# A four-layer graph network on one core: 166 loads moved to ScalarE's DMA queue, and four other orders of transfers and sums

## The chip, the cores and the metric

The kernel runs on one core of one Trainium2 chip. The metric is the device time of one execution in microseconds (us), taken as the median of several executions. Three executions of the kernel before gave 2234.57, 2238.84 and 2247.07 us.

The core's engines are TensorE (PE in the profile; PEld is its loading of weights), VectorE (DVE), ScalarE (ACT), GpSimd (POOL) and SyncE (SP). Each engine works through its own instructions in order. Transfers (DMAs) are started by instructions too: an engine that starts one only issues it, and 16 DMA engines move the bytes. In this kernel SyncE does nothing but issue transfers, GpSimd issues the others, and ScalarE, before the change, issues none.

## The reference

N = 2708 nodes, D = 512 features, `adj` a symmetric matrix of zeros and ones with about 16 ones in a row. Four layers, each in the form x = layernorm(x + layer(x)):

```python
deg = max(sum(adj != 0), 1)
x = ln(x + relu((dinv*(adj + I)*dinv @ x + x) @ W0 + b0))   # dinv = rsqrt(deg)
x = ln(x + (dis*adj*dis @ x) @ W1.T + b1)                   # dis = (deg + 1e-8)**-0.5
x = ln(x + gat(gat(x, W2[0]), W2[1]))
x = ln(x + adj @ (x @ W3 by heads) + b3)

def gat(x, W):
    Wh, Ws = split(x @ W, 2)
    a = softmax(Wh @ Ws.T, axis=-1) * adj
    return leaky_relu(a @ Wh + x)
```

The softmax runs over all 2708 columns, and only then is the result masked by `adj`, so the scores are needed in full but the product `a @ Wh` only where `adj` has ones.

## The kernel before, in words

**Tiling.** Nodes come in 22 blocks of 128 (the last has 20) and in six chunks of columns, four of 512, one of 384 and one of 276 (`CH`). The layers 0, 1 and 3 (class `Fast`) multiply by the adjacency: its bytes are loaded (`load_bytes`), ScalarE converts them to float (`m<-at` in the profile), and TensorE multiplies them with x (`acc<-m`). Attention (class `Attention`, L1632 ff.) works on scores transposed: for a chunk of 512, 384 or 276 queries it makes 22 tiles of scores, one for each block of keys.

**One chunk of attention.** `walk` (L2531) makes the scores. Chunks 0 to 3 of the first attention layer and 0 to 2 of the second do it by seven products instead of eight for two tiles (`pair_steps`, L2103): these need sums of halves of the weights (`s1`, `s2`, `s4`, kept in memory by `keep_sums` and loaded again by `load_sums`, L2047, tile group `s<-sums`) and sums of halves of the chunk's own columns (`t1`, `t2`, `t4`, made on VectorE by `sum_moving`, L2067). Their matmuls are `spx` and `spy`; ScalarE copies the results out of the accumulators into pages `s`, `u` and `v`, and VectorE adds them. The other chunks multiply plainly (`scores`, L2210, matmul `sp<-xs`). The chunk's own columns, four pages `xs`, are loaded by `load_moving` (L2200).

When a chunk's scores are there, the maximum is taken, and `soften` (L2306) is called once for each block while the next chunk's scores are made: VectorE subtracts the shift, ScalarE takes the exponential three blocks later, VectorE adds it to the sum and multiplies with the mask, and SyncE stores the tile to memory (`pairs<-s`). Mask bytes come by `load_mask` (L2291, `a<-mask`), four blocks (`DC`) in a page.

Then `fetch` (L2364) has GpSimd gather the few rows that each query needs (`g<-pairs,givers`, an indirect DMA), `weigh` sums them on TensorE (`acc<-g`), and `end` adds the query's own row `xr` (loaded by `load_rows`, L2391) and, in the second layer, the row `x` that the layer began with (`ch.first`, loaded in `fetch`).

**What sets the order.** `Attention.layer` (L2552) is an order written out by hand. The steps of a chunk are counted by n: at n = 15 the following chunk's `xs` are loaded, at n = 18 `sum_moving` is called for it, and `soften_next`, `greatest`, `weigh` and `copy_z` are spread over the steps. The first groups of the last layer (`early`, L645) run as filling in the tail of attention. A helper (`OrderedEngine`, L63) issues every instruction, so all have line L71 in the profile, and groups are told apart by their tiles. Instructions enter each engine's queue in the order of the program.

**Pages.** Nearly all tiles are pages of 2 KB in each of 128 partitions from one pool of 87. A page is used again when its last reader is done: a copy into a page that an earlier tile held waits for that tile's store to have read it. These waits, and those of a transfer for an earlier one with the same completion semaphore, are put in by the framework.

Of the kernel before, what the change touches and what calls it, by code (L numbers as in the profile page):

```python
# [12 lines left out]
U8 = mybir.dt.uint8  # L13
# [6 lines left out]
P = 128  # L20
N = 2708
D = 512
NB = 22
NP = NB * P
DC = D // P
BANK = 512
# [27 lines left out]
class Ordered:  # L54


    def __init__(self, tc):
        self.tc, self.last = tc, {}
        for name in ("tensor", "vector", "scalar", "gpsimd", "sync"):
            setattr(self, name, OrderedEngine(self, getattr(tc.nc, name)))  # L60
# [415 lines left out]
def blocks_of(k):  # L476

    c0, cw = CH[k]
    return [(c0 // P + q, q * P, min(P, cw - q * P)) for q in range(-(-cw // P))]
# [22 lines left out]
STREAMED = 4  # L502
# [8 lines left out]
def lists_of(i):  # L511

    if rows_of(i) <= QW:
        return [[QUARTERS * ONLY]] + [[t] for t in range(ONLY)]
    rest = [[QUARTERS * ONLY + t] for t in range(REST)]
    return rest + [[q * ONLY + t for q in range(QUARTERS)] for t in range(ONLY)]


def cost(columns):

    return 4 * columns / 2400
# [31 lines left out]
class Fast:  # L553
# [91 lines left out]
    def early(self, run):  # L645

        seq = run.seq
        yield True
        self.load(*seq[0])
        yield True  # L650
        self.load(*seq[1])
        self.prepare(*seq[0])
        yield True
        for t in range(4 * TWO):
            ly, k, g = seq[t]

            for later in seq[t + 2 if t == 0 else t + 6 : t + 7]:
                self.load_bytes(*later)
            if t < 2:
                self.attention.need(GROUPS[t + 2][1] - 1)  # L660
            if t == 1:
                for j in range(*GROUPS[3]):
                    ly.rows[j] = self.attention.made[j]
            self.load(*seq[t + 2])
            if t == 4:
                self.load_weights(ly)
            if t == 4 * TWO - 1:
                self.attention.need(GROUPS[4][1] - 1)
                for j in range(*GROUPS[4]):
                    ly.rows[j] = self.attention.made[j]  # L670
            self.prepare(*seq[t + 1])
            if g == 3:
                ly.begun[k] = []
            for n, j in enumerate(range(*GROUPS[g])):
                if t == 0:
                    self.multiply(ly, k, g, [j])
                else:
                    self.multiply(ly, k, g, ds=[n])
                if g == 3:
                    b = self.page(f"begun{k}_{n}")  # L680
                    self.nc.scalar.copy(b[:, : CH[k][1]], ly.acc[k][n][:, : CH[k][1]])
                    ly.begun[k].append(b)
                self.attention.advance(2 * cost(CH[k][1]))
                yield True
# [912 lines left out]
class Chunk:  # L1597


    def __init__(self, ly, k):  # L1600
        self.ly, self.k, self.cw = ly, k, CH[k][1]
        self.name = f"{ly.number}_{k}"
        self.blocks = blocks_of(k)
        self.s, self.masks, self.ends = {}, {}, []
        self.half = self.cw // 2
        self.seven = k in SEVEN[ly.number]
        self.part, self.complete, self.ready, self.top = {}, [], [], None
        self.softened = 0
        self.masks_ahead = 2 if k < STREAMED else 5
        self.fetched, self.rden = [], None  # L1610
        self.x, self.first = {}, {}
        self.rows = set()
        self.mv = None

        self.to_weigh = []
        for q, (i, _, _) in enumerate(self.blocks):
            ts = lists_of(i)
            self.to_weigh += [(q, t, t is ts[0], t is ts[-1]) for t in ts]
        self.to_fetch = [(q, t) for q, ts, _, _ in self.to_weigh for t in ts]
        self.first_fetch = self.to_fetch[0]  # L1620
# [11 lines left out]
class Attention:  # L1632
# [414 lines left out]
    def load_sums(self, ly, k):  # L2047

        for n, name in enumerate(("s1", "s2", "s4")):
            t = self.page(f"{name}_{ly.number}_{k}", FP, (P, 2, 2 * P))  # L2050
            self.nc.sync.dma_start(t, self.sums[ly.number][k][n])
            ly.sums[k][name] = [t[:, c, :] for c in range(2)]

    def replace(self, ly, k):
# [145 lines left out]
    def load_moving(self, ch):  # L2200

        ch.xt = []
        for c in range(DC):
            t = self.page(f"xs{ch.name}_{c}")
            self.nc.sync.dma_start(
                t[:, : ch.cw], self.k.turned[ch.ly.number][ch.k][:, c, :]
            )
            ch.xt.append(t)
# [80 lines left out]
        nc.scalar.copy(ch.shift[:, : ch.cw], ps[:, : ch.cw])  # L2289

    def load_mask(self, ch, g):  # L2291
        j0, j1 = g * DC, min((g + 1) * DC, NB)
        a = self.page(f"a{ch.name}_{j0}", U8, (P, DC, ch.cw))
        self.nc.sync.dma_start(a[:, : j1 - j0, :], self.k.masks[ch.k][:, j0:j1, :])
        for j in range(j0, j1):
            ch.masks[j] = a[:, j - j0, :]
# [9 lines left out]
    def soften(self, ch):  # L2306


        nc, v, cw = self.nc, ch.softened, ch.cw
        ch.softened += 1  # L2310
        if v < NB:
            n = rows_of(v)
            s = ch.s[v][:n, :cw]
            nc.vector.tensor_sub(s, s, ch.shift[:n, :cw])
        j = v - APART
        if 0 <= j < NB:
            s = ch.s[j][: rows_of(j), :cw]
            nc.scalar.activation(s, s, AF.Exp)
        j -= 1
        if j < 0:  # L2320
            return
        if j == NB - 1:
            ch.softened = SOFT
        if j == 0 and ch.k >= 2:
            while self.chunks[ch.k - 2].to_fetch:
                self.weigh(True)
        if j % DC == 0 and j + ch.masks_ahead * DC < NB:
            self.load_mask(ch, j // DC + ch.masks_ahead)
        n = rows_of(j)
        s = ch.s[j][:n, :cw]  # L2330
        if j == 0:
            ch.sum = self.page(f"sum{ch.name}")
            nc.vector.tensor_copy(ch.sum[:, :cw], s)
        else:
            nc.vector.tensor_add(ch.sum[:n, :cw], ch.sum[:n, :cw], s)
        nc.vector.tensor_mul(s, s, ch.masks.pop(j)[:n, :cw])
        to = ch.ly.pairs[ch.k % 2][j * P : j * P + n, :]
        if cw == BANK:
            four = [to.ap[0], (PAIR, 2), (P + D, 2), (1, P)]
            nc.sync.dma_start(  # L2340
                bass.AP(to.tensor, to.offset, four),
                ch.s[j][:n, :].rearrange("j (r b x) -> j r b x", r=2, b=2),
            )
            return
        nc.sync.dma_start(to[:, :P], ch.s[j][:n, :P])
        nc.sync.dma_start(to[:, P + D : D + cw], ch.s[j][:n, P:cw])
# [17 lines left out]
    def fetch(self, ch):  # L2364


        q, t = ch.to_fetch.pop(0)
        g = self.f.wide(f"g{ch.name}_{q}_{t}")
        i, _, w = ch.blocks[q]

        for b in (q, q + 1):
            self.load_rows(ch, b)
        if ch.ly.number == 1 and q not in ch.first:
            ch.first[q] = self.page(f"x1{ch.name}_{q}")
            self.nc.sync.dma_start(ch.first[q][:w], self.k.saved[1][i][:w])

        h = t // ONLY if t < QUARTERS * ONLY else (0, QUARTERS - 1)[q % 2]
        first, width = (P, D + (h + 1) * QW) if q % 2 else (h * QW, D + P - h * QW)
        self.nc.gpsimd.indirect_dma_start(
            out=g[:, :width],  # L2380
            out_offset=None,
            in_=ch.ly.pairs[ch.k % 2][:, :],
            in_offset=bass.IndirectOffsetOnAxis(ap=self.k.givers[:, i, t : t + 1], axis=0),
            element_offset=(q // 2) * PAIR + first,
        )

        begin = max(self.fetch_free, self.clock + (FIRST_LANDS if (q, t) == ch.first_fetch else 0))
        self.fetch_free = begin + 1.15
        ch.fetched.append((g, self.fetch_free + 6))

    def load_rows(self, ch, q):  # L2391
        if q in ch.rows or q >= len(ch.blocks):
            return
        ch.rows.add(q)
        i, _, w = ch.blocks[q]
        ch.x[q] = self.page(f"xr{ch.name}_{q}")
        given = self.k.saved[1] if ch.ly.number == 0 else self.k.between
        self.nc.sync.dma_start(ch.x[q][:w], given[i][:w])

    def fetch_ahead(self):  # L2400
        count = sum(len(c.fetched) for c in self.chunks)
# [150 lines left out]
    def layer(self, ly, chunks, fill):  # L2552
        f = self.f
        self.chunks, self.made = chunks, {}
        for k, ch in enumerate(chunks):
            old = chunks[k - 1] if k else None
            following = chunks[k + 1] if k + 1 < len(chunks) else None

            n = -1
            for what in self.walk(ch):  # L2560
# [22 lines left out]
                    f.packed(k - 1)  # L2583
                if following and n == 15:
                    self.load_moving(following)
                if following and following.seven and n == 18:
                    self.sum_moving(following)
                if not following and n in (5, 11, 19):
                    next(fill)
# [143 lines left out]
```

## Time and profile before

| | |
|---|---|
| median of three executions | 2238.84 us |
| profiled execution | 2238.97 us |
| its span in the trace | 2236.7 us (2.3 us lie outside) |
| matmuls, instructions in all | 10012, 30610 |
| transfers, moved | 310990 packets, 487.90 MB |
| mean granted TensorE clock | 0.992 |

A line of the page's first part gives each engine's busy us, its share of the span and its instructions. The stages are, from the trace: layers 0 and 1 to about 560 us; attention's projections, with the first chunk of scores, to about 800; its further chunks, the first scores from plain `xs` tiles at 801.9 and the last at 1888.3; gathers from 903.3 to 2030.0, the sums `acc<-g` to 2037.6; and the last layer to the end. Four of the groups that the change moves, by their tiles, with the number of transfers that SyncE issues: `s<-sums` 60, `xs<-t` 40, `xr<-x` and `xr<-y` 44, `x<-x` (in `fetch`) 22. SyncE issues 1224 transfers in all. Where a wait is shown, its columns are the engine, the tile that waited, the engine or transfer that ended the wait, us in total, times, and the longest.

### The profile page before, as it was taken

The numbers are of one execution on the slowest core, as the hardware profiler recorded it, in microseconds if no ns is written. First come the engines' busy times: TensorE is split into PE (matmuls) and PEld (weight loads), VectorE is DVE, ScalarE is ACT, GpSimd is POOL, SyncE is SP. The second block draws the span as 40 slices with busy tenths as digits, with TensorE's granted clock in tenths as the row PEclk, the third lists the DMA queues.
The fourth block names the chain that finished last, engine by engine and source line by source line (L and its number), as shares of the span: only waits on it lengthen the run. The fifth ranks groups of instructions, "written<-read, shape, count | busy, mean of one in ns | idle before, by whom it ended". The sixth has DMA issues, their size and how long they took to land.

```text
span 2236.7 us, 30610 instructions
## 1 busy us (share of the span) xinstructions
PE 2182.9 (98%) x10012; PEld 1576.6 (70%) x10012; DVE 1626.8 (73%) x3425; ACT 824.9 (37%) x1855; POOL 722.2 (32%) x827
## 2 busy tenths in 40 slices
PE   9999999999999999999999999999999998999997
PEld 6777788889887888765555666788743455577896
DVE  6777888897887869987758733459979698545744
ACT  7444363333333345433323422335423223342121
POOL 2333441111000000657465452000466666643000
PEclk9999999999999999999999999999999999999999
DMA  9976762222412855999799885674899899974221
GB/s 347 287 199 171 197 189 65 88 84 91 158 58 96 289 176 155 318 327 333 244 357 342 277 287 178 212 259 134 274 324 322 284 329 354 324 242 129 94 87 43
DMA packets 310990, 487.90 MB, mean 218 GB/s; under 512 B 37434, under 2 KB 178010, under 8 KB 310820
## 3 DMA queue, kind: packets, MB, share of 16 engines
q1 hardware_dynamic: 242164, 270.69, 36.5%
q0 software_dynamic: 68656, 215.15, 29.3%
q8 instruction: 81, 1.33, 0.2%
q14 instruction: 89, 0.73, 0.1%
HBM read 356.23 MB, written 162.76 MB: 232 GB/s over the span
## 4 chain that ended last, share of the span: by engine, by line
PE 94%; DVE 2%; issue 1%; DMA 1%; another core or an unknown queue 1%; ACT 0%; DVEq 0%; ACTq 0%; POOL 0%; POOLq 0%
PE acc L71 39%; PE sp L71 13%; PE spx L71 10%; PE spy L71 7%; PE mm L71 4%; PE mmx L71 3%; PE mmy L71 2%; PE z_0x L71 2%; PE wst L71 2%; PE z_0y L71 1%; PE mix L71 1%; PE wst_0x L71 1%; PE wst_1x L71 1%; PE z_1x L71 1%; PE wst_0y L71 1%
## 5 line engine op out<-in xcount | busy, mean ns | idle before, releaser
L71 POOL DMA_INDIRECT g<-pairs,givers x510 | 540.1, 1059 | 808.0 <-DMA xr<-x 235.3
L71 PE MATMUL acc<-m,xh 128*128 128x512 f32 (+4 forms) x1584 | 562.1, 376 | 6.7 <-ACT s L71 6.7
L71 PE MATMUL acc<-m,xl 128*128 128x512 f32 (+4 forms) x1584 | 548.1, 364 | 0.3 <-issue 0.3
L71 PEld LDWEIGHTS acc<-m,xh 128*128 128x128 f32 (+1 forms) x1584 | 287.4, 188 | 64.3 <-issue 17.2
L71 PEld LDWEIGHTS acc<-m,xl 128*128 128x128 f32 (+1 forms) x1584 | 287.7, 188 | 42.4 <-issue 3.6
L71 PE MATMUL sp<-xs,wst_sb 128*128 128x384 f32 (+2 forms) x960 | 301.5, 486 | 0.1
L71 PE MATMUL acc<-g 128*32 128x512 f32 (+1 forms) x1020 | 273.1, 613 | 7.2 <-issue 4.1
L71 PEld LDWEIGHTS sp<-xs,wst_sb 128*128 128x128 f32 x960 | 166.4, 183 | 133.0 <-issue 74.4
L71 ACT CAST m<-at 128x512 fp32r<-128x512 uint8 (+5 forms) x396 | 201.8, 569 | 111.4 <-DMA at<-mask 47.9
L71 DVE TENSOR_TENSOR sum<-sum,s 128x512 f32<-128x512 f32 (+4 forms) x252 | 156.9, 623 | 30.2 <-ACT s L71 22.9
L71 DVE TENSOR_TENSOR s<-s,a 128x512 f32<-128x512 f32 (+3 forms) x264 | 166.1, 629 | 9.1
L71 PEld LDWEIGHTS acc<-g 128*32 128x32 f32 (+1 forms) x1020 | 77.9, 136 | 134.4 <-issue 105.9
L71 DVE TENSOR_TENSOR top<-top,s 128x512 f32<-128x512 f32 (+3 forms) x240 | 149.4, 623 | 26.2 <-issue 15.3
L71 DVE TENSOR_TENSOR s<-s,shift 128x512 f32<-128x512 f32 (+3 forms) x264 | 161.2, 619 | 1.6 <-issue 1.3
L71 ACT COPY s<-sp 128x384 f32<-128x384 f32 (+2 forms) x112 | 52.5, 473 | 291.3 <-PE sp L71 153.9
L71 ACT ACTIVATE s<-s 128x512 f32<-128x512 f32 (+3 forms) x264 | 146.8, 581 | 13.5 <-DVE s L71 8.4
L71 POOL DMA_DIRECT2D x<-o x44 | 25.7, 590 | 325.2 <-DVE o L71 281.8
L71 ACT COPY s<-spx 128x256 f32<-128x256 f32 x210 | 77.5, 373 | 136.7 <-PE spx L71 98.1
L71 PE MATMUL spx<-xs,wst_sb 128*128 128x256 f32 x400 | 103.2, 383 | 0.0
L71 PE MATMUL mm<-w,ht 128*128 128x512 f32 (+1 forms) x240 | 99.1, 594 | 0.0
L71 DVE SCALAR_TENSOR_TENSOR xr<-acc,rden,xr 128x512 f32<-128x512 f32 (+1 forms) x44 | 32.8, 746 | 84.6 <-PE acc L71 65.2
L71 PEld LDWEIGHTS spx<-xs,wst_sb 128*128 128x128 f32 x400 | 76.0, 191 | 19.5 <-issue 7.4
(349 smaller groups left out, 3331.0 us busy)
## 6 DMA issues: line engine op xcount, KB each, us to landing
pairs<-s SPq DMA_DIRECT2D x168, 256.0 KB
at<-in_adj_t SPq DMA_DIRECT2D x84, 256.0 KB
pairs<-pairs SPq DMA_DIRECT2D x42, 512.0 KB
s<-sums SPq DMA_DIRECT2D x60, 256.0 KB
xres<-x POOLq DMA_DIRECT2D x44, 256.0 KB
x<-o POOLq DMA_DIRECT2D x43, 256.0 KB
pairs<-z_sb SPq DMA_DIRECT2D x42, 256.0 KB
pairs<-pairs SPq DMA_DIRECT2D x42, 256.0 KB
```

The source lines that it names most:

```text
L71: ins = call(*args, **kw)
```

## The change

It makes five edits.

- Four loads are issued in ScalarE's queue rather than SyncE's, at the same places of the program: the sums (`load_sums`), the chunk's columns (`load_moving`), the rows (`load_rows`) and the second layer's first rows (in `fetch`). That is 166 transfers.
- A mask page holds as many blocks as fit in it: four for chunks of 512, five for 384, seven for 276.
- The number of mask pages loaded ahead in chunks 4 and 5 goes from five to all but one: four and three.
- `early` loads the bytes of the last layer four groups ahead rather than six.
- `sum_moving` is called at n = 20, the last step of a chunk, rather than at n = 18.

```diff
         for t in range(4 * TWO):
             ly, k, g = seq[t]
-            for later in seq[t + 2 if t == 0 else t + 6 : t + 7]:
+            for later in seq[t + 2 if t == 0 else t + 4 : t + 5]:
                 self.load_bytes(*later)
...
-        self.masks_ahead = 2 if k < STREAMED else 5
+        self.together = BANK * DC // self.cw
+        self.masks_ahead = 2 if k < STREAMED else -(-NB // self.together) - 1
...
             t = self.page(f"{name}_{ly.number}_{k}", FP, (P, 2, 2 * P))
-            self.nc.sync.dma_start(t, self.sums[ly.number][k][n])
+            self.nc.scalar.dma_start(t, self.sums[ly.number][k][n])
...
             t = self.page(f"xs{ch.name}_{c}")
-            self.nc.sync.dma_start(
+            self.nc.scalar.dma_start(
                 t[:, : ch.cw], self.k.turned[ch.ly.number][ch.k][:, c, :]
             )
...
-        j0, j1 = g * DC, min((g + 1) * DC, NB)
-        a = self.page(f"a{ch.name}_{j0}", U8, (P, DC, ch.cw))
+        j0, j1 = g * ch.together, min((g + 1) * ch.together, NB)
+        a = self.page(f"a{ch.name}_{j0}", U8, (P, ch.together, ch.cw))
...
-        if j % DC == 0 and j + ch.masks_ahead * DC < NB:
-            self.load_mask(ch, j // DC + ch.masks_ahead)
+        if j % ch.together == 0 and j + ch.masks_ahead * ch.together < NB:
+            self.load_mask(ch, j // ch.together + ch.masks_ahead)
...
-            self.nc.sync.dma_start(ch.first[q][:w], self.k.saved[1][i][:w])
+            self.nc.scalar.dma_start(ch.first[q][:w], self.k.saved[1][i][:w])
...
-        self.nc.sync.dma_start(ch.x[q][:w], given[i][:w])
+        self.nc.scalar.dma_start(ch.x[q][:w], given[i][:w])
...
-                if following and following.seven and n == 18:
+                if following and following.seven and n == 20:
                     self.sum_moving(following)
```

## The prediction

> **What bounds the kernel now.** I read the page's busy shares first, then TensorE's waits, then the stage windows, then the places where TensorE stood still. The busy shares:
>
> ```profile
> span 2236.7 us, 30610 instructions
> PE 2182.9 (98%) x10012; PEld 1576.6 (70%) x10012; DVE 1626.8 (73%) x3425; ACT 824.9 (37%) x1855; POOL 722.2 (32%) x827
> ```
>
> TensorE is busy for all but 53.8 us of the span. The change touches no matmul, so that is the most that it can win directly. A second, smaller purse hangs on it: the granted clock stands at 0.5 for 6.8 us from 956.4, 1062.2, 1628.8 and 1895.1 and for 3.4 us from 1253.4, each time at a TensorE gap of 2.5 to 6.7 us. A window at half clock does half its work, so these cost about 4 x 3.4 + 1.7 = 15.3 us.
>
> TensorE's waits, columns: what waited, for what, us in total, times, longest:
>
> ```profile
> PE acc L71 <- ACT s L71: 6.7, 1, 6.7
> PE spx L71 <- issue: 5.7, 2, 4.9
> PE spx L71 <- ACT v L71: 4.8, 2, 3.9
> PE spy L71 <- issue: 4.6, 1, 4.6
> PE acc L71 <- issue: 4.4, 6, 1.4
> PE acc L71 <- DMA g<-pairs,givers: 2.7, 2, 1.8
> ```
>
> They are few and long. The windows (busy us and count of each engine, clock, DMA share, GB/s) tell where: 40 of the 54 us lie between 930 and 1990, in attention with its gathers.
>
> ```profile
> 930.00:1990.00 1060.00, 1020.46 (x4150) 646.59 (x4147) 748.60 (x1428) 360.05 (x814) 499.33 (x474) 0.99 0.85 287
> ```
>
> The 16 DMA engines are 85% busy here. I followed each gap to what ended it, in the rows of TensorE, ScalarE and SyncE, and sort them into three kinds:
>
> - **Stores that land late.** One at 1631.0 (4.60 us), and 0.74, 0.28 and 0.90 us at 1002.1, 1592.0 and 1602.7: 6.5 us, with 3.4 us of half clock after the first. In the timeline of SyncE, ScalarE and TensorE (start, duration, last idle time and releaser):
>
> ```profile
> 1617.71 7.88 SPq L71 DMA_DIRECT2D pairs<-s  x3
> ...
> 1630.58 0.37 ACT L71 COPY s<-spy 128x256 f32<-128x256 f32 x1 [10.51 <-DMA pairs<-s]
> ...
> 1631.01 2.07 PE L71 MATMUL spy<-xs,wst_sb 128*128 128x256 f32 x4 [4.60 <-issue]
> ```
>
> ScalarE's copy needs a page that `pairs<-s` is still reading; SyncE issued that store at 1617.71, after four `xs<-t`, an `xr<-y` and an `x<-x` (1611.52 to 1617.40), and in that stretch one issue of SyncE took 4.86 us. ScalarE idled 10.5 us and TensorE 4.6 of them: it had some 5.9 us of other work in hand, gather products among it.
> - **Gathers that come late**, 946.5, 1035.8, 1165.3, 1920.3, 1929.6: 0.92 + 0.57 + 1.07 + 1.44 + 1.81 = 5.8 us.
> - **Late signals.** At 957.6, 1063.3, 1253.2, 1314.6, 1317.3, 1363.4 and 1897.3 the matmul had ended, by its record, up to 10 us before ScalarE's copy began, with no other releaser in the trace: with smaller ones about 25 us, and 3 x 3.4 + 1.7 = 11.9 us of half clock. (Normally the copy follows 36 ns behind.) No part of the change is aimed at them.
>
> ScalarE's own waits for transfers, the edge that the change works on:
>
> ```profile
> ACT s L71 <- DMA pairs<-s: 15.4, 5, 10.5
> ...
> ACT v L71 <- DMA pairs<-s: 10.6, 4, 6.5
> ...
> ACT s L71 <- DMA a<-mask: 7.7, 3, 3.5
> ...
> ACT s L71 <- DMA xs<-t: 4.4, 2, 3.8
> ```
>
> **The moved loads: what SyncE gains.** 60 `s<-sums`, 40 `xs<-t`, 44 `xr` and 22 `x<-x` go to ScalarE's queue: 166 issues. By their rows an issue takes 0.40 to 0.47 us, say 166 x 0.45 = 75 us less of SyncE and 75 us more in ScalarE's queue. SyncE's time is not itself on the path: its longest waits are for results of VectorE (300.1 us for `s`). What counts is that stores no longer stand behind loads. In the 4.60 us case six loads stood ahead; a 256 KB load is 0.45 us of issue and, at the stage's 287 GB/s, about 0.9 us of transfer (estimates from these rows). I take the **late stores as gone: -6.5 - 3.4 = -9.9 us** (bounds -9.9 and 0), and the **late gathers as gone, -5.8** (bounds -5.8 and 0), since a gather starts only when the store before it has landed.
>
> Against this stands a bandwidth reading: from 1628 to 1636 the DMA engines are full (share 1.06), so that a load on another queue still takes the same engines. The Trainium skill says so too ("DMA: Bandwidth & Descriptors", section "Issuing engines are not separate DMA queues"): transfers started by different engines share the 16 DMA engines, and issuing from several saves only issue time. By it the two terms would be near 0 and the time 2239 plus ScalarE's cost; the row of 1617.71, where issue and order on SyncE are late in themselves, is why I don't go by it alone.
>
> **What ScalarE loses.** In the built programs the transfers of SyncE and ScalarE take eight completion semaphores in turn. So a load in ScalarE's queue waits for the transfer about eight earlier in program order, mostly a `pairs<-s`, a mask or a `pairs<-pairs` of SyncE, and ScalarE's copies and exponentials stand behind it; SyncE's next stores wait likewise for the loads, which are issued earlier, so that this way round costs little. In exchange 118 fewer of ScalarE's copies and exponentials wait for a transfer themselves (573 to 455). The trace of before shows no load on ScalarE, so I put each at its new place in ScalarE's order and looked up when the transfer that it would wait for landed before: ScalarE is held 75 us in 64 places, mostly in idle time that it has anyway. Blocks of over 7 us stand at 921.0 (11.0), 941.9 (7.1), 1151.7 (8.5), 1183.6 (9.6), 1278.0 (8.2), 1309.7 (7.9), 1619.5 (11.5), and at 1903.5 and 1972.4 where ScalarE has nothing to do. Followed on to TensorE (a product is 0.86 us; without gather products ScalarE has three products less a 0.37 us copy = 2.2 us of grace), ten of them reach it: 0.45 + 3.06 + 4.29 + 1.01 + 2.50 + 0.08 + 5.37 + 3.55 + 2.75 + 0.35 = 23.4 us. That is the upper end, with stores landing as they did behind 166 loads. Below nothing is excluded: a block only delays. The relief worked out above is 1.35 us for each load gone from ahead of a store; with two to six gone that is 2.7 to 8 us, as long as most of these blocks. So I take **+5 us** (bounds 0 and 23.4, to which four gaps of over 3 us could add 1.7 to 3.4 us of half clock each).
>
> **Mask pages.** Chunks of 384 columns go from six mask loads to five, of 276 from six to four: 6 issues of about 0.4 us off SyncE, which is not on the path, and one page and two pages fewer held. Each load is larger (up to 242 KB for 138 KB), issued three or four pages ahead. ScalarE's 7.7 us for `a<-mask` bound it: between -7.7 and +7.7 on ScalarE, of which TensorE sees a quarter (6.5 of 26.0 for the stores); I take **0**.
>
> **Bytes of the last layer, four groups ahead.** They are used later than they land by tens of us (`at3_1_2` landed at 1912 and is converted at 1961); the pages are free longer. **0**; if the cover were gone, a copy `m<-at` would wait a landing of 4.6 to 8.7 us once or twice.
>
> **Moving sums two steps later.** Six VectorE subtractions of 0.42 us for each of five chunks, with no transfers. The first chunk's end at 796.1 and are used at 807.1: 11 us of cover, less two steps (one pair, 6.05 us) leaves 5. **0**; without cover 2.5 us for each chunk, 12.7 in all. In exchange VectorE's chain of softmax goes on two steps longer undisturbed.
>
> **Sum.** 2238.97 - 9.9 - 5.8 + 5 = 2228.3; the profiled execution stands 0.13 us over the median, so **2228 us**. Its own spread, by the half of each term, is 2218 to 2236.
>
> **The rivals.** A difference of about 0.5% (11 us) is what can be told from no change here.
>
> *ScalarE blocked (slower).* The loads' waits for semaphores hold the copies, and TensorE pays what I followed to it: 2238.97 + 23.4 + two half clocks of 3.4 - 9.9 = 2259. It decides from the point at which half of the ten blocks are paid. For it: one block of ScalarE's queue in before (10.51 us) cost TensorE 4.6 us and half clock. Against it: of 26.0 us that ScalarE waited for stores TensorE saw 6.5.
>
> *Hidden anyway (no change).* Transfers are the limit (0.85 and 1.06 of the engines), stores land as before, ScalarE's blocks fall in its idle time: 2234 to 2243, 2239 at the middle. For it: SyncE's idle time, 300 us behind VectorE's `s` alone. This is also the case in which the change doesn't do what its words say.
>
> *Late signals move.* They are 25 + 11.9 us and depend on what falls together; if half go, 2228 - 18 = 2210; if they grow by half the case looks like the first rival.
>
> **How the numbers follow.** Forecast 0.45, ScalarE blocked 0.27, hidden 0.18, late signals fewer 0.10. Faster by over 0.5% (below 2227.6): over half of the first, all of the last, a little of the third: 0.38. Slower (above 2250): most of the second and the tail of the others: 0.28. Within: 0.34. Range 2206 to 2260: from the last rival's time to the ScalarE rival's.
>
> **What would show it.** Right: ScalarE's waits for `pairs<-s` shrink below 10 us, no gap of TensorE follows a store, gathers wait under 2 us. Wrong: ScalarE's idle time before copies ends at a DMA issue of its own queue, with TensorE gaps near 921, 941, 1151, 1278 or 1309; or the gaps of the first two kinds stay with the same sizes. If late signals differ by 15 us or more the forecast fails by a term that I set to 0.

## The result, and the profile after

The changed kernel takes 2271.34 us (median of five, 2261.77 to 2276.43), 1.0125 times the kernel before (95% interval 1.0096 to 1.0155): slower, and above the range of the forecast. Its profiled execution took 2271.34 us with a span of 2268.9 us. The page's first part after:

```profile
span 2268.9 us, 30484 instructions
PE 2192.1 (97%) x10012; PEld 1580.1 (70%) x10012; DVE 1626.1 (72%) x3425; ACT 822.8 (36%) x1855; POOL 715.0 (32%) x827
```

The span is 32.2 us longer. TensorE's busy time grew by 9.2 us, with the same 10012 matmuls, and its idle time by 23.0 (76.8 for 53.8). The first is the granted clock: without the window at the kernel's end it now stands at 0.5 for 61.2 us, where it stood for 30.6. In these windows TensorE was busy for 43.1 us, before for 23.9; half of the 19.2 more is 9.6, close to the 9.2. The second is in TensorE's waits (what waited, for what, us, times, longest):

```profile
PE wst_0x L71 <- ACT wst_sb L71: 10.3, 1, 10.3
PE acc L71 <- DMA g<-pairs,givers: 9.3, 5, 6.4
PE acc L71 <- issue: 9.2, 9, 2.4
PE spx L71 <- ACT v L71: 9.1, 3, 7.0
```

The two waits for ScalarE of 10.3 and 7.0 us are ahead of matmuls that had no gap before. ScalarE was busy 822.8 us in 2268.9, so it was not short of time. The window of the gathers holds less matmul work than before (4013 matmuls for 4150), with less clock (0.97 for 0.99) and no more DMA share (0.82 for 0.85):

```profile
930.00:1990.00 1060.00, 999.65 (x4013) 629.49 (x4014) 728.24 (x1381) 348.61 (x792) 481.73 (x462) 0.97 0.82 279
```

What ScalarE did is in its timeline at the 10.3 us wait. The columns are start, duration, engine, operation, tiles, and in brackets the idle time before and what ended it; ACTq is ScalarE's queue issuing a transfer:

```profile
1283.45 0.43 ACT L71 ACTIVATE s<-s 128x276 f32<-128x276 f32 x1 [0.83 <-DVE s L71]
1294.81 0.33 ACTq L71 DMA_DIRECT2D xr<-x  x1
1295.18 0.43 ACT L71 ACTIVATE s<-s 128x276 f32<-128x276 f32 x1 [11.29 <-DMA xt<-t]
1295.52 0.35 ACT L71 COPY wst_sb<-wst_0y 128x256 f32<-128x256 f32 x1
1295.77 0.38 ACT L71 COPY wst_sb<-wst_0x 128x256 f32<-128x256 f32 x1
```

The copies `wst_sb` have nothing to do with `xr<-x`. Their matmuls had ended at 1282.3 and 1283.2. But they stand behind the load in ScalarE's queue, and the load stands until a transfer of SyncE, `xt<-t`, has landed at 1294.8. SyncE issued it in this group:

```profile
1286.01 5.50 SPq L71 DMA_DIRECT2D xt<-t  x8
```

In the built program the load needs nothing of that `xt`. The two share a completion semaphore, which the `xt` had eight transfers earlier in the turn: the trace has number 101 for both, and the `xt` is the third of the eight, issued at 1287.04. The chain of work that ended last has the landing as one of its longest pieces, and two `pairs<-s` besides, the first of them behind `xr0_0_2` (start, us, what):

```profile
926.53 7.73 DMA pairs<-s
...
1003.36 7.20 DMA pairs<-s
...
1287.04 7.75 DMA xt<-t
```

The second place is the one that the prediction put at 921.0:

```profile
920.24 7.09 ACTq L71 DMA_DIRECT2D xs<-t  x3
934.29 0.33 ACTq L71 DMA_DIRECT2D xr<-x  x1
934.65 0.37 ACT L71 COPY v<-spx 128x256 f32<-128x256 f32 x1 [13.92 <-DMA pairs<-s]
```

The copy `v<-spx` comes 13.9 us after ScalarE's last work, and TensorE loses 7.03 us at 935.1.

I followed every gap of TensorE of over 0.25 us (without the one at the kernel's start), as before, and sorted them (us):

| | before | after |
|---|---|---|
| behind a load in ScalarE's queue | 0 | 22.7 |
| a store landed late | 6.5 | 0 |
| a gather came late | 6.6 | 10.9 |
| late signals and the rest | 26.9 | 28.7 |
| sum | 40.0 | 62.3 |

The 22.7 are at 935.1 (7.03), 1296.2 (10.27), 1503.5 (1.93) and 1637.7 (3.47). A gap of 2.78 us at 1331.3 is not one of them, though two loads stand ahead of it: they were issued by 1323.8 without a wait, and ScalarE's copy began at 1330.69 on a late signal, as at 1314.6 in the kernel before. The gathers before are 6.6 rather than the prediction's 5.8, which left out 0.81 us at 1167.5. By my count over the rows, which no single view shows, ScalarE's next copy or exponential started 104.9 us later than its inputs and ScalarE's own work allowed, summed over 65 places where loads stood ahead of it.

### The profile page after: what moved, and what is told of

It reads as the page before. It is cut to its first block, busy times and chain, and to the rows that moved or that the text cites. A ratio compares the mean times of both kernels' runs of the same rounds, so it can differ in the third digit from the quotient of the medians.

```text
span 2268.9 us, 30484 instructions
## 1 busy us (share of the span) xinstructions
PE 2192.1 (97%) x10012; PEld 1580.1 (70%) x10012; DVE 1626.1 (72%) x3425; ACT 822.8 (36%) x1855; POOL 715.0 (32%) x827
## 3 DMA queue, kind: packets, MB, share of 16 engines
q1 hardware_dynamic: 217738, 229.31, 30.5%
## 4 chain that ended last, share of the span: by engine, by line
PE 89%; DMA 4%; DVE 4%; issue 2%; POOL 0%; ACT 0%; another core or an unknown queue 0%; SPq 0%; ACTq 0%; DVEq 0%
PE acc L71 38%; PE sp L71 13%; PE spx L71 8%; PE spy L71 6%; PE mm L71 4%; PE mmx L71 3%; PE mmy L71 2%; DVE s L71 2%; PE z_0x L71 2%; PE wst L71 2%; PE mix L71 1%; PE z_0y L71 1%; PE wst_0x L71 1%; DMA g<-pairs,givers 1%; PE wst_1x L71 1%
## 5 line engine op out<-in xcount | busy, mean ns | idle before, releaser
L71 POOL DMA_INDIRECT g<-pairs,givers x510 | 533.7, 1046 | 843.3 <-DMA a<-mask 243.3
L71 DVE TENSOR_TENSOR s<-s,shift 128x512 f32<-128x512 f32 (+3 forms) x264 | 161.1, 619 | 12.7 <-ACT shift L71 12.6
```

The source lines that it names most:

```text
L71: ins = call(*args, **kw)
```

## The experiments

Theory A: ScalarE stands behind its own loads, which wait for a shared semaphore, and TensorE pays. The rivals: B, the moved bytes delay stores and gathers; C, it is chance, or the other edits; D, the semaphores' turns cost SyncE as much as ScalarE. Runs of one group shared a chip and the runs of the kernel before; medians of different groups are not to be compared, ratios are.

### First group: which part, and the queue by itself (before: 2241.79 us)

**The moves alone** (before, with the four `dma_start` of the loads changed):

```diff
-            self.nc.sync.dma_start(t, self.sums[ly.number][k][n])
+            self.nc.scalar.dma_start(t, self.sums[ly.number][k][n])
...
```

> The kernel before with the 166 loads in ScalarE's queue and nothing else of the change. Theory A (ScalarE stands behind its loads, which wait for a semaphore of an earlier store, and TensorE pays): the whole loss is here, 2260 to 2278 us. Theory B (the transfers of the second queue take bandwidth from stores and gathers, so that these land later; ScalarE's queue itself costs little): the same. Theory C (the loss is of late signals that fall together by chance, or of the masks, the bytes and the sums): 2234 to 2250.

Measured: 2272.94 us, ratio 1.0161 (1.0132 to 1.0191). The whole loss is in the moves. TensorE's gap behind the same load, `xr0_4_2`, is 10.68 us here. But one late store is back too, 6.59 us at 1011.4: the relief that the changed kernel's trace shows for stores isn't regular.

**The rest alone** (the changed kernel with the four loads on `nc.sync` again).

> The changed kernel with all 166 loads back in SyncE's queue: masks, bytes and the moving sums are as changed. A and B: 2232 to 2245 us, within 0.5% of before. C: 2255 to 2275.

Measured: 2242.76 us, 1.0015 (0.9995 to 1.0035). Mask pages, bytes and the moving sums are worth nothing that can be measured; C's second half falls.

**Rows back** (the changed kernel, two of four back):

```diff
-        self.nc.scalar.dma_start(ch.x[q][:w], given[i][:w])
+        self.nc.sync.dma_start(ch.x[q][:w], given[i][:w])
...
```

> The changed kernel with the 66 loads of rows (xr, x) back in SyncE's queue, the 100 of sums and columns left in ScalarE's. A: the gaps of TensorE at 935, 1331 and most of that at 1637 end, some 13 us, with their half clock of some 8 us: 2246 to 2256 us. B: the rows are 40% of the bytes moved, so some 40% of the loss goes, 2256 to 2261. C: no clear difference to the changed kernel, 2262 to 2276.

Measured: 2256.17 us, 1.0073 (1.0049 to 1.0098). The edge between A's and B's numbers, so the time alone doesn't decide; the trace does: no gap at 1296 is left and 0.60 us of that at 935 (behind columns), and the others behind loads stand behind sums (803.3, 1496.4, 1601.1: some 2 us each). I also put 953.7 (1.98 us) behind sums; its row has a late signal.

**Transfers of 64 bytes on ScalarE.** Everything else as before:

```diff
+    def tiny(self):
+        n = self.tinies = getattr(self, "tinies", -1) + 1
+        self.nc.scalar.dma_start(self.k.aside[n : n + 1, :], self.k.ident[:1, :16])
...
             self.nc.sync.dma_start(t, self.sums[ly.number][k][n])
+            self.f.tiny()
```

> The kernel before with all its loads in SyncE's queue and, beside each of the 166, a transfer of 64 bytes issued by ScalarE to memory that nothing reads. It takes part in the turns of completion semaphores as the moved loads do, but carries no bytes and relieves SyncE of nothing. A: ScalarE is held as in the changed kernel, 2255 to 2285 us, with TensorE's gaps behind ScalarE's copies near 935, 1331, 1503 or 1637. B and C: 2234 to 2246.

Measured: 2259.56 us, 1.0089 (1.0063 to 1.0116). No load is moved, no bytes are worth speaking of, and still it is slower, at the same place and by the same transfer:

```profile
1274.96 0.43 ACT L71 ACTIVATE s<-s 128x276 f32<-128x276 f32 x1 [0.83 <-DVE s L71]
1287.88 0.20 ACTq L71 DMA_DIRECT2D aside<-ident  x1
1288.13 0.43 ACT L71 ACTIVATE s<-s 128x276 f32<-128x276 f32 x1 [12.73 <-DMA xt<-t]
```

TensorE, next to it, lost more than in the changed kernel:

```profile
1289.15 2.08 PE L71 MATMUL wst_0x<-xt,s3mixed 128*128 128x256 f32 x4 [11.95 <-ACT wst_sb L71]
```

A transfer of 64 bytes that nobody needs held ScalarE for 12.7 us. B can't explain that. The 166 of them cost 0.9% where the moves cost 1.6.

### Second group: who issues, and each part by itself (before: 2210.52 us)

**The same 64 bytes on SyncE** (`self.nc.sync` in `tiny`).

> The kernel before with the same 166 transfers of 64 bytes beside the loads, issued by SyncE and not by ScalarE. They take the same turns of completion semaphores, and SyncE's queue grows by 166 issues, but ScalarE issues nothing. Theory A (ScalarE stands behind what it issues): 2236 to 2248 us, no gap of TensorE of over 7 us but those of before. Theory D (166 more turns of the eight semaphores keep fewer stores under way, whoever issues): as the run with ScalarE's tiny transfers, 2254 to 2268.

Measured: 2211.27 us, 1.0000 (0.9990 to 1.0010). With 166 issues more on SyncE the time stands still. D falls on this chip, and with it the price of SyncE's issue time: these issues took 48.7 us of SyncE in the trace, and cost nothing.

**Each kind of load alone** on ScalarE, in the kernel before: the 60 sums, the 40 columns, the 66 rows (in each case the one or two `dma_start` of the change).

> The kernel before with the 60 loads of sums alone in ScalarE's queue. A: the gaps behind these loads as with the rows back (803, 953, 1496, 1601: 8 us) and their half clock of some 6 us, so 2250 to 2258 us. B (bytes): a third of the loss, 2249 to 2253. If they are free: 2236 to 2245.

Measured: 2223.27 us, 1.0062 (1.0046 to 1.0078). Theory A explains little of this one. The two gaps behind loads are 1.15 and 2.03 us. The two longest, 10.30 us at 953.3 and 5.68 at 1011.3, are late stores: ScalarE's copy itself waits for a page that `pairs<-s` is still reading, and no load stands between:

```profile
952.89 0.37 ACT L71 COPY s<-spx 128x256 f32<-128x256 f32 x1 [12.88 <-DMA pairs<-s]
```

SyncE issued that store at 941.00, just after an `xs<-t` whose semaphore it shares had landed (940.93), and from 941 to 953 the DMA engines were full (share 1.06). The late store near 1011 is also in the moves alone (6.59 us), with the rows back (3.05) and with one load back (7.27, below): kernels with the sums on ScalarE, though the two traces of the changed kernel have no such gap. Whether the moved bytes (B) or the changed order of the turns makes these stores late was not tried.

> The kernel before with the 40 loads of the chunk's columns alone in ScalarE's queue. A: with the rows back no gap stood behind them, so 2236 to 2246 us, or below 2236 if SyncE's relief at the fifteenth step is worth what the prediction took for it. B: a quarter of the bytes, 2246 to 2251.

Measured: 2203.54 us, 0.9967 (0.9954 to 0.9980), a gain, of 7 us.

> The kernel before with the 66 loads of rows alone in ScalarE's queue. A: the gaps of over 7 us near 935 and 1296 with their half clock, some 25 us, and little else: 2256 to 2268 us. B: 40% of the bytes, 2251 to 2256.

Measured: 2221.10 us, 1.0050 (1.0037 to 1.0063). Its trace has three gaps behind loads of rows, 3.67, 8.45 and 6.40 us; the second is again `xr0_4_2`:

```profile
PE wst_0x L71 <- ACT wst_sb L71: 8.5, 1, 8.5
PE spx L71 <- ACT v L71: 6.4, 1, 6.4
```

Sums and rows cost less than I expected from the other chip's gaps. By the same count as above, the time that ScalarE's ready work was held is 19.6 us with the sums, 30.5 with the columns and 62.8 with the rows, so the hold alone doesn't order the three times: with columns alone little of it reached TensorE (one gap, 2.33 us).

### Third group: one load, and other queues (before: 2247.95 us)

**The changed kernel again.**

> The changed kernel as it is, for the two runs beside it. If the parts add up as on the chip of the single parts (sums 13 us, columns -7, rows 11), 1.008 times the kernel before, some 17 us; if as on the first chip, 1.012 to 1.016.

Measured: 2281.91 us, 1.0159 (1.0128 to 1.0190). This is the ratio that the moves alone had in the first group; whether the parts add up on the chip of the second wasn't run.

**One load of 166 back:**

```diff
-        self.nc.scalar.dma_start(ch.x[q][:w], given[i][:w])
+        nc = self.nc.sync if ch.name + str(q) == "0_42" else self.nc.scalar
+        nc.dma_start(ch.x[q][:w], given[i][:w])
```

> The changed kernel with one load of 166 back in SyncE's queue: xr0_4_2, behind which ScalarE stood until the load xt2_1_2_2 of SyncE had landed. A: TensorE's gap of 8 to 11 us before wst1_1_0x goes, and the half clock after it (up to 5 us): 9 to 16 us less than the changed kernel beside it. B: one load of 256 KB moves nothing, within 3 us of it.

Measured: 2273.69 us, 1.0124 (1.0088 to 1.0160): 8.2 us below the run beside it, just under A's range; the two intervals overlap, so the time alone shows little. In the trace the gap is gone. The changed kernel of this group, TensorE:

```profile
1304.50 2.07 PE L71 MATMUL wst_0x<-xt,s3mixed 128*128 128x256 f32 x4 [6.44 <-ACT wst_sb L71]
```

With the one load back, the same matmul and its copies, with no idle time ahead of the matmul:

```profile
1299.11 1.13 PE L71 MATMUL wst_0x<-xt,s3mixed 128*128 128x256 f32 x4
```

```profile
1296.27 0.43 ACT L71 ACTIVATE s<-s 128x276 f32<-128x276 f32 x1 [0.76 <-DVE s L71]
1296.61 0.35 ACT L71 COPY wst_sb<-wst_0y 128x256 f32<-128x256 f32 x1
1296.86 0.38 ACT L71 COPY wst_sb<-wst_0x 128x256 f32<-128x256 f32 x1
```

TensorE's idle time is 15.0 us less in this trace than in the one beside it (71.9 for 86.9). The gap is 6.44 of that; the rest is other places, among them a late signal of 8.35 us at 1352.3 that only the changed kernel's trace has.

**Columns on ScalarE, rows on GpSimd, sums on SyncE** (the changed kernel, `nc.gpsimd` for the two loads of rows, `nc.sync` for the sums).

> The changed kernel with the sums back in SyncE's queue and the rows in GpSimd's, right ahead of the gathers that need them; columns in ScalarE's. A: no load is left in ScalarE's queue that it stood behind, SyncE issues 106 fewer: at or below the kernel before, ratio 0.990 to 1.000. If GpSimd's gathers wait behind the rows: TensorE's waits for g grow by more than 5 us and the ratio is over 1.003.

Measured: 2254.91 us, 1.0031 (1.0009 to 1.0054). Not a gain: the trace has a gap of 7.17 us behind the last `xs1_3` in ScalarE's queue at 1621.4, and late gathers sum to 9.2 us. My expectation that nothing would stand behind columns was wrong.

**All 166 on GpSimd** (`nc.gpsimd` for `nc.scalar` in all four).

> The changed kernel with all 166 loads in GpSimd's queue instead of ScalarE's. SyncE is relieved by the same issues and the bytes go by another queue all the same, but ScalarE stands behind nothing. A: the gaps behind ScalarE's copies go; what GpSimd's waiting for gathers does to sums and columns comes instead, and would show as TensorE or VectorE waiting for those loads; without it ratio 0.990 to 1.003. B: as the changed kernel, over 1.008, with late stores and gathers.

Measured: 2293.49 us, 1.0221 (1.0187 to 1.0255), the slowest. No copy of ScalarE is held, but the sums now stand behind GpSimd's gathers and what those wait for, and TensorE waits for them itself:

```profile
PE spy L71 <- DMA s<-sums: 33.6, 3, 14.0
PE acc L71 <- DMA g<-pairs,givers: 7.9, 7, 4.7
```

The same mechanism on another queue: a load is as late as what it stands behind. It doesn't speak on B.

### Fourth group: the two queues side by side (before: 2249.44 us)

> 166 transfers of 64 bytes on ScalarE beside the loads, as before, for the run beside it. A: ratio 1.006 to 1.013. D (the turns of the semaphores alone): the same as the run on SyncE beside it.

Measured: 2265.56 us, 1.0081 (1.0055 to 1.0108).

> The same 166 transfers on SyncE. A: ratio 0.997 to 1.003, clear of the run on ScalarE. D: no clear difference to it.

Measured: 2252.95 us, 1.0031 (1.0010 to 1.0051). Clear of ScalarE's run, so the place of the issue counts, as A has it. But the interval lies above 1: on this chip more turns alone cost 0.1 to 0.5%, so a part of D stands.

> The 40 loads of columns alone on ScalarE. If the relief of SyncE is worth something whatever the chip: ratio 0.994 to 0.999, with less waiting for stores than before. If ScalarE's holds of 4 to 9 us behind these loads eat it on a slower chip: 1.000 to 1.004.

Measured: 2254.06 us, 1.0013 (0.9991 to 1.0035). The gain of the columns alone on the chip of the second group is not seen on this one. No kernel here was faster than the kernel before on both chips.

## Why the prediction was wrong, step by step

Between the forecast of -10.7 us and the 32.2 us by which the span grew lie 42.9 us: 17.7 are ScalarE's holds (22.7 for 5), 12.6 the half clock (9.2 for -3.4), 10.1 the gathers (4.3 for -5.8), and 2.5 late signals and small gaps.

**The step that failed** is "So I take +5 us (bounds 0 and 23.4, to which four gaps of over 3 us could add ...)", the price of ScalarE standing behind its loads. The mechanism was named there, and so were most of its places. The placement gave 75 us of hold in 64 places; my count in the trace is 104.9 in 65. It gave ten places that reach TensorE with 23.4 us; the trace has four with 22.7. The sum agrees better than the places do: of the blocks of over 7 us that I listed, 921.0 became a gap of 7.03 us, 1278.0 one of 10.27 and 1619.5 one of 3.47, while 941.9, 1151.7, 1183.6 and 1309.7 reached nothing. What I set against it was wrong: "The relief worked out above is 1.35 us for each load gone from ahead of a store". The load at 1294.8 shows why. It waits for a transfer that SyncE issued at 1287.04 as the third of eight `xt<-t`, and no moved load stood just ahead of these. Where semaphores tie a load to what SyncE did eight transfers ago, taking other loads off SyncE doesn't bring that landing forward. With 23.4 for 5 the sum would have been 2246.7 us, and with the half clock that I named beside it, up to 13.6 us, 2260.

**The half clock** was counted as half of each window. Windows grew by 30.6 us, TensorE's busy time by 9.2, so a window cost 0.3 of its length: TensorE is idle in part of it (43.1 of 61.2 us busy), and half of its busy time there fits. The prediction's 15.3 us for the windows before would be 12 by that.

**What SyncE gains.** The -6.5 for late stores did come in the profiled execution (no such gap), but a run with the same moves has one of 6.59 us again, and the sums alone have 10.30 and 5.68. The -5.8 for gathers went the other way: 10.9 us for 6.6, +4.3. In the chain of work, the worst one (6.37 us at 1942.1) follows the landing of an `x<-x` at 1935.37, and that an `a<-mask` at 1932.41; SyncE issued both, so no moved load is in that piece. The direct measure of SyncE's issue time is the pair of runs that add 166 issues to it: 1.0000 and 1.0031. The Trainium skill's rule ("DMA: Bandwidth & Descriptors", section "Issuing engines are not separate DMA queues"), that another issuing engine saves only issue time, agrees with these two numbers; I had set it aside for the one row at 1617.71. That row's stall was of order in the queue, and the change moved the order problem to an engine that TensorE waits for.

**Mask pages, bytes, moving sums** at 0: right, 1.0015 (0.9995 to 1.0035).

**Late signals** at 0: right in sum, 26.9 and 28.7 us with the rest, though at other places.

**The rival** "ScalarE blocked", 2259 us at 0.27, is what happened, 12 us dearer than I priced it: its 23.4 for TensorE's gaps was right (22.7), but half clock came to 9.2 us where it had 3.4 in all, gathers to 4.3 and late signals and small gaps to 2.5 where it had nothing. The range ended at its middle, 2260, and so left out all that could go worse in that very case.

**What stays open.** The transfers of 64 bytes on ScalarE cost 0.8 to 0.9%, of which 0.3 came on SyncE too on one of two chips; the real loads cost 1.25 to 1.6%. By my count ready work of ScalarE was held 94 and 102 us with the one and 105, 117 and 128 with the other, which is part of the difference. The rest isn't separated: loads that take part in the turns for longer (SyncE's waits for `pairs<-s` are 28.7 us in 16 after, 4.8 in 9 before), or their bytes; the late stores of the runs with sums on ScalarE belong here. That a load would be free on ScalarE without the shared semaphores wasn't tried.

## What to carry to other kernels

In these runs the issue of a transfer stands in its engine's order like any other instruction: what it waits for, everything behind it on that engine waits for too (12.7 us for 64 bytes). Before loads go to a compute engine's queue, list for each what its completion semaphore last served and when that lands; if the engine feeds the bottleneck within a few us, leave the loads on an engine that feeds nothing. And when the placement of single instructions gives a loss, don't discount it by an average relief: ask at its largest places whether the relief touches that very wait.

## What the runs showed of the hardware that I had not expected

The kernel before takes 2210.52 us in the second group and 2241.79, 2247.95 and 2249.44 in the others, 17 to 23 executions each. In the four traces of the second group there is no late signal that cost TensorE over 0.5 us, while each trace of the other groups has some 9 to 25 us of them by my sorting (a matmul ended, ScalarE's copy some us later, no other releaser). Two kernels ran on both sides: 64 bytes on SyncE has none of them on the one chip and 18 us on the other, the columns alone none and 24 us. So, as far as one trace of each tells, this loss goes with the chip that ran and not with the kernel. What delays the signal isn't shown.
